# Cross-attention on one core: where the first products of a seven-product block stand against their sums, the order of some loads, and who does the two last steps

## The chip, the cores and the metric

The kernel runs on one core of one Trainium2 chip. A core has a matrix engine, TensorE (PE in the profile, its weight loads PEld), and three engines for everything else: VectorE (DVE), ScalarE (ACT) and GpSimd (POOL). The fifth, SyncE (SP), issues nearly all the DMA transfers here. Each engine works through its own list of instructions in order and waits on semaphores for the others. The metric is the device time in microseconds (us) of one execution.

## The reference, cut to what matters

There are 64 independent blocks. For each, `x` is 256 rows of 512 and the context `c` 256 rows of 384, all in fp32; the weights are shared.

```python
text_p  = x @ W_text  + b_text                   # 256 x 512
audio_p = c @ W_audio + b_audio                  # 256 x 512
Q = layer_norm(text_p,  g1, beta1)
K = layer_norm(audio_p, g2, beta2)
alpha = softmax(Q @ K.T / sqrt(512))             # 256 x 256
h = (alpha @ audio_p) @ W_out + b_out            # 256 x 512
out = layer_norm(h + x, g_out, beta_out)
```

## The kernel before

The kernel does not form `alpha @ audio_p` with the projected context. It multiplies `alpha` with the rows of `c` (the result is called z), and `W_audio @ W_out`, worked out once at the start (`wao`), does the rest; the biases are likewise folded into one row `bao`. A block so has five pieces of work for TensorE: q (x to queries), k (c to keys), sc (scores), z (exponentials times c) and y (z times `wao`).

The pieces q, k and y are done by `Blocks`: a product of matrices cut in two by two is made from seven products of half size, with sums of operands ahead (`sum_x`, `sum_c`, on GpSimd: `xsum`, `csum`, `zsum`; `weight_sums` for the weights) and sums of results behind. Seven products go to four PSUM banks: (1, 6), (2, 5), (3, 4) and (7). `products(...)` issues the matmuls, `leave(...)` issues the sums by which VectorE takes a product out of its bank (line 490): `leave(1)` reads the half bank of product 1, `leave(6)` that of product 6, `leave(2, 5)` and `leave(3, 4)` a whole bank each. Where the program has `leave(1)` ahead of product 6, product 6, which writes to the same bank, waits for that sum. A matmul of fp32 operands is issued in two passes, so a product over one chunk of 128 is two entries of the profile.

The order of work is written out by hand: the scheduler is off (`manual_schedule`), so each engine's instructions stand in the order in which the program calls them. Before the loop, block 0 is projected in the plain way (`Projection`) and block 1 by `Blocks`, among the work on the weights. The last lines there are, in this order: `q[1].products(1, 2)`, `leave(1)`, the turn of q[0], its scaling (`affine`), the other products and sums of q[1], the rest of the weights' work, and the store and re-fetch of q[1].

The loop runs over b from 0 to 61. In iteration b the kernel does the scores of block b, q and k of block b + 2 (held in `q2` and `k2`), z and y of block b - 1 (`last`), and the output layer norm of block b - 2 (`done`). [...]To turn a matrix the kernel loads it in squares of 32 (`squares`, four DMAs, line 88) and lets VectorE transpose the squares (`turn`, line 91, and line 442 for keys). For x and c that is a load from the inputs (`load_x`, `load_c`: `xq`, `cq`; issued in iteration b for block b + 4, and turned by `turn_next(b + 3)`); the queries, keys and exponentials are first written to memory (`qd`, `kd`, `ed`) and fetched back as squares (`qq`, `kq`, `eq`). `turn_e` turns the exponentials. `load_rows(b + 1)` loads block b + 1's x and c as rows: c for z, x for the residual sum `add_x`, which comes two iterations after that block's scores. All these DMAs stand in SyncE's one queue; the rows `go` and `beo` (`g_out` and `beta_out` over all partitions) are loaded through it ahead of the loop.

Buffers bind the order further: most SBUF tiles have two buffers, the x and c rows three, and PSUM's eight banks are six in a ring for products (`p_pj`) and two for scores and z (`p_at`).

After the loop the blocks 62 and 63 are finished by hand, in a stretch in which the exponentials of the last two are turned by TensorE and not through memory (`transpose_e`), and y is made by plain matmuls (`multiply`, `multiply_halves` for the last tile). There the layer norm is: `evict` (VectorE: multiply by the reciprocal of the softmax sum, add x, take mean and variance, lines 638, 267, 268), `scales` (GpSimd: add epsilon, line 344, and raise to the power of -1/2, line 346), `shift` (VectorE: subtract the mean, multiply by `go`, line 704) and `settle` (VectorE: multiply by the scale, add `beo`, line 709; `settle_halves`, line 692, for the last tile), then `store` (line 719, or 695 for the halves).

Of the kernel before, what the change touches and what calls it, by code (L numbers as in the profile page):

```python
# [9 lines left out]
F32 = mybir.dt.float32  # L10
AF = mybir.ActivationFunctionType
ALU = mybir.AluOpType
# [3 lines left out]
P = 128  # L16
SQ = 32
NQ = P // SQ
EPS = 1e-05
# [3 lines left out]
def kernel(  # L23
# [41 lines left out]
    nc = tc.nc  # L65
    ctx.enter_context(tc.manual_schedule())
    B, L, D = x.shape
    S, DA = c.shape[1:]
    H = w_text.shape[1]
    LT, ST = L // P, S // P  # L70
# [4 lines left out]
    xin = ctx.enter_context(tc.tile_pool(name="xin", bufs=3))  # L75
# [20 lines left out]
    def load_c(b):  # L96
        cq = blk.tile([P, S // SQ, DA // NQ], F32, tag="cq", name=f"cq_{b}")
        squares(cq, c[b])
        blocks[b] = [cq]

    def load_x(b):
        xq = blk.tile([P, L // SQ, D // NQ], F32, tag="xq", name=f"xq_{b}")
        squares(xq, x[b])
        blocks[b].append(xq)

    def load_squares(b):
        load_c(b)
        load_x(b)

    def load_rows(b):  # L110
        x_sb = xin.tile([P, LT, D], F32, tag="x", name=f"x_{b}")
        c_sb = cin.tile([P, ST, DA], F32, tag="c", name=f"c_{b}")
        nc.sync.dma_start(x_sb, x[b].rearrange("(t p) d -> p t d", p=P))
        nc.sync.dma_start(c_sb, c[b].rearrange("(t p) d -> p t d", p=P))
        return x_sb, c_sb

    ident = const.tile([P, P], F32, tag="ident", name="ident")
    make_identity(nc, ident)
# [13 lines left out]
    def row(v, name):  # L132
        t = const.tile([P, H], F32, tag=name, name=name)
        nc.sync.dma_start(t, v.rearrange("(o h) -> o h", o=1).broadcast_to([P, H]))
        return t
# [4 lines left out]

    x_0 = xin.tile([P, LT, D], F32, tag="x", name="x_0")
    c_0 = cin.tile([P, ST, DA], F32, tag="c", name="c_0")
    c_rows, x_rows = [v[0].rearrange("(t p) d -> p t d", p=P) for v in (c, x)]
    wa_sb = const.tile([P, AC, H], F32, tag="wa", name="wa")
    wt_sb = const.tile([P, DC, H], F32, tag="wt", name="wt")

# [2 lines left out]
        for q in range(NQ):  # L149
            queues[q].dma_start(t[q * SQ : (q + 1) * SQ, lo : lo + n], v[q, :, lo : lo + n])  # L150

    nc.sync.dma_start(c_0[:, :1], c_rows[:, :1])
    weight_chunks(wa_sb, w_audio, 0, 1, [nc.scalar, nc.sync, nc.scalar, nc.sync])
    weight_chunks(wa_sb, w_audio, 1, 2, [nc.sync] * NQ)
    nc.sync.dma_start(c_0[:, 1:], c_rows[:, 1:])
    for t in range(LT):
        nc.sync.dma_start(x_0[:, t, :], x_rows[:, t, :])
    weight_chunks(wt_sb, w_text, 0, 2, [nc.sync] * NQ)
    ba_sb = row(b_audio, "ba")
    weight_chunks(wt_sb, w_text, 2, 2, [nc.sync] * NQ)  # L160
# [123 lines left out]
    H2 = H // 2  # L284
# [53 lines left out]
    def rstd_of(var, n, total=False):  # L338

        ve = small.tile([P, n], F32, tag="ve", name="ve")  # L340
        if total:
            nc.gpsimd.tensor_scalar(ve, var, 1.0 / D, EPS, ALU.mult, ALU.add)
        else:
            nc.gpsimd.tensor_scalar(ve, var, EPS, None, ALU.add)  # L344
        r = small.tile([P, n], F32, tag="rstd", name="rstd")
        nc.gpsimd.tensor_tensor(r, ve, nhalf[:, :n], ALU.pow)  # L346
        return [r[:, t : t + 1] for t in range(n)]
# [157 lines left out]
    class Attention:  # L505
        def __init__(self, b):
            self.b, self.qT, self.kT = b, q.pop(b).T, k.pop(b).T
            self.xb, self.c_sb = rows[b]

        def scores(self, end=False):  # L510
            if end:
# [84 lines left out]

        def add_x(self):
            for t in range(LT):
                nc.gpsimd.tensor_tensor(self.y[:, t, :], self.y[:, t, :], self.xb[:, t, :], ALU.add)  # L599

        def statistics(self):

# [34 lines left out]
        def evict(self, t):  # L637
            nc.vector.scalar_tensor_tensor(  # L638
                self.y[:, t, :],
                self.ps_y.pop(t),  # L640
                self.rden[:, t : t + 1],
                self.xb[:, t, :],
                ALU.mult,
                ALU.add,
            )
            moments(self.mv, self.y[:, t, :], t)

        def scales(self, lo=0, n=LT):
            self.r = getattr(self, "r", {})
            self.r.update({lo + t: r for t, r in enumerate(rstd_of(self.mv[:, lo : lo + n, 1], n))})  # L650

        def moments(self, tiles=range(LT)):
            if 0 in tiles:
# [20 lines left out]
        def evict_halves(self, t):  # L674
            st = small.tile([P, 2, 6], F32, tag="st2", name="st2")
            for h in range(2):
                half = self.y[:, t, bass.ts(h, H2)]
                nc.vector.scalar_tensor_tensor(
                    half,
                    self.ps_h[h],  # L680
                    self.rden[:, t : t + 1],
                    self.xb[:, t, bass.ts(h, H2)],
                    ALU.mult,
                    ALU.add,
                )
                nc.vector.bn_stats(st[:, h, :], half)
            nc.vector.bn_aggr(self.mv[:, t, :], st)
# [46 lines left out]
    def turn_next(b):  # L734
        xT[b] = turn_x(b)
        xs[b] = sum_x(xT.pop(b))
        cT[b] = turn_c(b)
        cs[b] = sum_c(cT.pop(b))

    def add_bias(b):  # L740
        xb = rows[b][0]
        for t in range(LT):
            nc.gpsimd.tensor_tensor(xb[:, t, :], xb[:, t, :], bao_sb, ALU.add)

    assert B > 3
    q, k, xT, cT, rows = {}, {}, {}, {}, {0: (x_0, c_0)}


    c_turn = RowTurn(c_0, AC, "cT")
# [77 lines left out]
    k[0].affine(g2_sb, be2_sb)  # L827
    part = bias_parts()
    q[1] = Blocks("q", 1, xs.pop(1), wt_blocks, bt_sb)
    q[1].products(1, 2)  # L830
    q[1].leave(1)
    q[0].turn()
    q[0].affine(g1_sb, be1_sb)
    q[1].products(6, 5)
    q[1].leave(6)
    q[1].leave(2, 5)
    q[1].products(3, 4)
# [13 lines left out]
    q[1].normalise()  # L851
    q[1].store()
    q[1].fetch()
    go_sb = row(g_out, "go")
    beo_sb = row(beta_out, "beo")

    done = last = None
    for b in range(B - 2):
        three = b + 3 < B
        at = Attention(b)  # L860
        at.scores()
        if done:
            done.o.leave(3, 4)
            done.o.leave(7)
            done.add_x()
        if last:
            last.turn_e()
        if three and b:
            turn_next(b + 3)
        at.maxima()  # L870
        at.exponentials()
        if not b:
            k[1].turn()
        q2 = q[b + 2] = Blocks("q", b + 2, xs.pop(b + 2), wt_blocks, bt_sb)
        q2.products(1, 6)
        q2.leave(1)
        q2.leave(6)
        at.reciprocals()
        at.divide_e()
        if not b:  # L880
            k[1].affine(g2_sb, be2_sb)
        if b:
            q[b + 1].fetch()
            k[b + 1].fetch()
        at.store_e()
        if b + 4 < B:
            load_squares(b + 4)
        at.fetch_e()
        rows[b + 1] = load_rows(b + 1)
        if done:  # L890
            done.statistics()
        q2.products(2, 5)
        q2.leave(2, 5)
        q2.products(3, 4)
        q2.leave(3, 4)
        q2.products(7)
        q2.leave(7)
        q2.square()
        q2.scales()
        q[b + 1].turn()  # L900
        if not b:
            turn_next(3)
        if done:
            done.shift(0)
            done.shift(1)
        if last:
            last.context()
        q[b + 1].affine(g1_sb, be1_sb)
        if b:
            k[b + 1].turn()  # L910
            k[b + 1].affine(g2_sb, be2_sb)
        if done:
            done.settle(0)
            done.settle(1)
            done.store()
        q2.normalise()
        q2.store()
        if last:
            last.start_products()
        k2 = k[b + 2] = Blocks("k", b + 2, cs.pop(b + 2), wa_blocks, ba_sb)  # L920
        k2.products(1, 6)
        k2.leave(1)
        k2.leave(6)
        k2.products(2, 5)
        k2.leave(2, 5)
        k2.products(3, 4)
        k2.leave(3, 4)
        k2.products(7)
        k2.leave(7)
        k2.square()  # L930
        k2.scales()
        k2.normalise()
        k2.store()
        if last:
            last.o.products(1, 6)
            last.o.leave(1)
            last.o.leave(6)
            last.o.products(2, 5)
            last.o.leave(2, 5)
            last.o.products(3, 4)  # L940
            last.o.products(7)
        done, last = last, at
# [2 lines left out]
    at = Attention(B - 2)  # L945
    q[B - 1].fetch()
    k[B - 1].fetch()
    rows[B - 1] = load_rows(B - 1)
    at.scores()
    done.o.leave(3, 4)  # L950
    done.o.leave(7)
# [11 lines left out]
    add_bias(B - 1)  # L963
    at.transpose_e()
    at.copy_e()
    last.o.products(1, 2)
    q[B - 1].turn()
    last.o.leave(1)
    last.o.products(4)
    q[B - 1].affine(g1_sb, be1_sb)  # L970
    k[B - 1].turn()
    last.o.products(6, 5)
    last.o.leave(6)
    last.o.leave(2, 5)
    k[B - 1].affine(g2_sb, be2_sb)
    done.settle(0)
    last.o.products(3)
    last.o.leave(3, 4)
    last.o.products(7)
# [23 lines left out]
    at.multiply(1)  # L1003
    at.shift(0)
    at.evict(1)
    at.scales(1, 1)
    at.settle(0)
    end.context()
    end.start_output()
    end.multiply(0)  # L1010
    at.shift(1)
    at.settle(1)
    at.store()
    end.evict(0)
    end.scales(0, 1)
    end.multiply_halves(1)
    end.shift(0)
    end.evict_halves(1)
    end.scales(1, 1)
    end.shift(1)  # L1020
    end.settle(0)
    end.store(0, 1)
    end.settle_halves(1)

# [31 lines left out]
```

## Time and profile before

| what | us |
|---|---|
| median of 3 runs (lowest, highest) | 1424.07 (1423.77, 1424.16) |
| the profiled execution, its own time | 1425.29 |
| its span in the profile | 1423.5 |
| PE busy | 1407.9 |
| DVE busy | 1232.9 |
| ACT busy | 932.8 |
| POOL busy | 875.9 |

One execution was profiled; the sums below are made from it. Its own time is 1.8 us more than its span, and 1.2 us more than the median of the runs. A row of the timeline gives the start, the time from the first to the last of the merged instructions, the engine, the line, the operation with output and inputs, and in brackets how long the engine was idle before it and what ended that. The chain of waits is followed back from the last instruction, and shows which engine's work set the end. The granted clock is the share of full speed that TensorE's clock gate let through. Ends of matmuls are modelled by the profile, and GpSimd's times are rough.

### The profile page before, as it was taken

How to read it: one execution, taken by the hardware profiler on the slowest of the kernel's cores; microseconds unless marked ns; L12 is line 12 of the kernel's file. 1: busy time of each engine (PE TensorE's matmuls, PEld its weight loads, DVE VectorE, ACT ScalarE, POOL GpSimd, SP SyncE). 2: the span in 40 equal slices, each digit the busy share in tenths (PEclk: the TensorE clock that was granted, in tenths of full speed). 3: DMA queues.
4: the chain of work that ended last, by engine and by line, in shares of the span. 5: the costliest groups of instructions: out<-in, count | busy, mean ns of one | idle time of the engine just before them, and what ended most of it. 6: DMA issues, size and time to landing. Idle time of an engine off the chain costs nothing.

```text
span 1423.5 us, 22648 instructions
## 1 busy us (share of the span) xinstructions
PE 1407.9 (99%) x6441; PEld 1223.2 (86%) x6441; DVE 1232.9 (87%) x1758; ACT 932.8 (66%) x2293; POOL 875.9 (62%) x1295
## 2 busy tenths in 40 slices
PE   9899999999999999999999999999999999999997
PEld 5688888888888888888888888888888888888885
DVE  5688988988889889889889889888888898898888
ACT  4576766766766766766766767667667667667662
POOL 4566576576566566666666665765665666666645
PEclk9999999999999999999999999999999999999999
DMA  8797788888877887887787887888888778788763
GB/s 195 190 263 236 228 228 238 237 226 236 241 221 231 225 240 233 222 239 234 216 247 231 220 245 230 223 243 237 219 240 244 218 234 236 225 235 231 221 191 116
DMA packets 450578, 322.57 MB, mean 227 GB/s; under 512 B 154900, under 2 KB 382996, under 8 KB 450452
## 3 DMA queue, kind: packets, MB, share of 16 engines
q1 hardware_dynamic: 450356, 320.98, 79.4%
q8 instruction: 52, 0.85, 0.3%
q14 instruction: 74, 0.61, 0.2%
q10 hardware_dynamic: 96, 0.13, 0.0%
HBM read 204.09 MB, written 116.92 MB: 226 GB/s over the span
## 4 chain that ended last, share of the span: by engine, by line
PE 97%; DVE 1%; DMA 1%; POOL 0%; issue 0%; ACT 0%; POOLq 0%; SPq 0%; DVEq 0%
PE ps_q L478 27%; PE ps_k L478 21%; PE ps_y L478 21%; PE ps_sc L517 16%; PE ps_z L583 11%; PE ps_wao L245 1%; PE ps_q L365 1%; DMA c<-in_ctx_dram 0%; DVE part L233 0%; DMA wa<-in_L_xattn_W_audio_dram 0%; PE ps_k L365 0%; DVE st L267 0%; DVE y L638 0%; POOL ve L344 0%; POOL rstd L346 0%
## 5 line engine op out<-in xcount | busy, mean ns | idle before, releaser
L490 DVE TENSOR_TENSOR qr<-ps_q,qr 128x512 f32<-128x512 f32 x252 | 174.2, 691 | 93.9 <-PE ps_q L478 91.5
L517 PE MATMUL ps_sc<-kT,qT 128*128 128x256 f32 x1024 | 231.5, 379 | 0.0
L344 POOL TENSOR_SCALAR ve<-var 128x2 f32<-128x2 f32 x126 | 43.9, 348 | 296.3 <-ACT junk L383 296.3
L517 PEld LDWEIGHTS ps_sc<-kT,qT 128*128 128x128 f32 x1024 | 194.6, 190 | 26.8 <-issue 0.5
L534 ACT ACTIVATE e<-ps_sc,nmx 128x256 f32<-128x256 f32 x128 | 59.5, 469 | 232.6 <-DVE nmx L527 232.6
L478 PE MATMUL ps_q<-wtsum,xsum 128*128 128x256 f32 x756 | 195.7, 382 | 4.7 <-DVE qr L490 4.7
L599 POOL TENSOR_TENSOR yr<-yr,x 128x512 f32<-128x512 f32 x124 | 155.9, 1280 | 71.1 <-DVE yr L490 71.1
L490 DVE TENSOR_TENSOR kr<-ps_k,kr 128x512 f32<-128x512 f32 x252 | 174.3, 692 | 22.5 <-DVE kr L490 0.9
L490 DVE TENSOR_TENSOR yr<-ps_y,yr 128x512 f32<-128x512 f32 x248 | 171.5, 692 | 22.0 <-DVE yr L490 0.9
L478 PE MATMUL ps_k<-wa,cT 128*128 128x256 f32 x630 | 177.1, 379 | 0.0
L583 PE MATMUL ps_z<-eT,c 128*128 128x256 f32 x768 | 176.5, 379 | 0.1
L478 PE MATMUL ps_y<-wao,zT 128*128 128x256 f32 x620 | 174.1, 379 | 0.0
L346 POOL TENSOR_TENSOR rstd<-ve,nhalf 128x2 f32<-128x2 f32 (+1 forms) x194 | 159.4, 821 | 16.1
L478 PEld LDWEIGHTS ps_q<-wtsum,xsum 128*128 128x128 f32 x756 | 144.7, 192 | 24.9 <-issue 5.0
L583 PEld LDWEIGHTS ps_z<-eT,c 128*128 128x128 f32 x768 | 145.9, 190 | 20.7 <-ACT e L534 0.5
L449 ACT ACTIVATE qT<-qT,columns 128x256 f32<-128x256 f32 x256 | 132.8, 591 | 5.8 <-DVE qT L91 5.8
L478 PEld LDWEIGHTS ps_k<-wa,cT 128*128 128x128 f32 x630 | 119.6, 190 | 16.2
L449 ACT ACTIVATE kT<-kT,columns 128x256 f32<-128x256 f32 x256 | 132.1, 587 | 1.4 <-DVE kT L91 1.1
L478 PEld LDWEIGHTS ps_y<-wao,zT 128*128 128x128 f32 x620 | 117.7, 190 | 15.9
L411 ACT ACTIVATE kr<-kr,rstd 128x512 f32<-128x512 f32 x126 | 84.1, 714 | 70.5 <-POOL rstd L346 70.5
L383 ACT ACTIVATE junk<-kr 128x512 f32<-128x512 f32 x126 | 79.4, 630 | 77.1 <-DVE kr L490 72.7
L709 DVE SCALAR_TENSOR_TENSOR yr<-yr,rstd,beo 128x512 f32<-128x512 f32 x124 | 128.7, 1075 | 0.6 <-POOL rstd L346 0.6
(150 smaller groups left out, 2980.7 us busy)
## 6 DMA issues: line engine op xcount, KB each, us to landing
kd<-kr SPq DMA_DIRECT2D x64, 512.0 KB, 3.1
kq<-kd SPq DMA_DIRECT2D x256, 128.0 KB, 3.3
qd<-qr SPq DMA_DIRECT2D x64, 512.0 KB, 4.4
qq<-qd SPq DMA_DIRECT2D x256, 128.0 KB, 3.3
xq<-in_x_dram SPq DMA_DIRECT2D x252, 128.0 KB, 3.0
x<-in_x_dram SPq DMA_DIRECT2D x63, 512.0 KB, 4.0
out_dram<-yr SPq DMA_DIRECT2D x62, 512.0 KB, 4.8
cq<-in_ctx_dram SPq DMA_DIRECT2D x252, 96.0 KB, 2.4
```

The costliest lines, as they stand in the source:

```text
L344: nc.gpsimd.tensor_scalar(ve, var, EPS, None, ALU.add)
L346: nc.gpsimd.tensor_tensor(r, ve, nhalf[:, :n], ALU.pow)
L383: nc.scalar.activation(junk, self.rows[:, t, :], AF.Square, scale=1.0 / math.sqrt(H), accum_out=self.var[:, t : t + 1],)
L411: nc.scalar.mul(row, row, self.r[t])
L449: nc.scalar.activation(self.T[:, k, :], self.T[:, k, :], AF.Identity, bias=bet[:, k : k + 1], scale=gam[:, k : k + 1],)
L478: nc.tensor.matmul(place, lhsT=side, rhs=w, start=(i == 0), stop=(i == len(pairs) - 1))
L490: add = lambda o, i0, i1: nc.vector.tensor_tensor(o, i0, i1, ALU.add)
L517: nc.tensor.matmul(self.sc[:, t, :], lhsT=self.qT[:, k, bass.ts(t, P)], rhs=self.kT[:, k, :], start=(k == 0), stop=(k == HC - 1),)
L534: nc.scalar.activation(self.e[:, t, :], self.sc[:, t, :], AF.Exp, bias=self.nmx[:, t : t + 1], accum_out=self.den[:, t : t + 1],)
L583: nc.tensor.matmul(ps[:, j, :], lhsT=self.c_sb[:, s, bass.ts(lo + j, P)], rhs=self.eT[:, s, :], start=(s == 0), stop=(s == ST - 1),)
L599: nc.gpsimd.tensor_tensor(self.y[:, t, :], self.y[:, t, :], self.xb[:, t, :], ALU.add)
L709: nc.vector.scalar_tensor_tensor(self.y[:, t, :], self.y[:, t, :], self.r[t], beo_sb, ALU.mult, ALU.add)
```

## The change

Five things change.

1. For q[1] ahead of the loop, and for the y of block 61 after it, all products of the first two banks are issued before the first sum. TensorE's order of matmuls stays as it was; what changes is which sums stand ahead of which product in the program. VectorE's order changes with it: the turn of q[0] now stands ahead of the sums of q[1]; after the loop, the turn of the last keys stands ahead of the first sum, and `done.settle(0)` ahead of that turn.
2. In the loop, `turn_next` stands ahead of `last.turn_e`.
3. In iteration 0 the squares of the exponentials are fetched ahead of `load_x`, and behind it in the later iterations as before.
4. x's rows of block b are loaded in iteration b and not in b - 1; the last iteration loads two blocks' rows. The loads of `go` and `beo` move from ahead of the loop into iteration 1.
5. At the end, `scales` of a single tile becomes `scale_soon`, where VectorE adds epsilon and GpSimd does the power alone (three times), and two of the `settle` become `settle_beside`: ScalarE multiplies by the scale and GpSimd adds `beo`.

```diff
-    def load_rows(b):
-        x_sb = xin.tile([P, LT, D], F32, tag="x", name=f"x_{b}")
-        c_sb = cin.tile([P, ST, DA], F32, tag="c", name=f"c_{b}")
-        nc.sync.dma_start(x_sb, x[b].rearrange("(t p) d -> p t d", p=P))
-        nc.sync.dma_start(c_sb, c[b].rearrange("(t p) d -> p t d", p=P))
-        return x_sb, c_sb
+    def load_x_rows(b):
+        x_rows[b] = xin.tile([P, LT, D], F32, tag="x", name=f"x_{b}")
+        nc.sync.dma_start(x_rows[b], x[b].rearrange("(t p) d -> p t d", p=P))
+
+    def load_c_rows(b):
+        c_rows[b] = cin.tile([P, ST, DA], F32, tag="c", name=f"c_{b}")
+        nc.sync.dma_start(c_rows[b], c[b].rearrange("(t p) d -> p t d", p=P))
...
+        def scale_soon(self, t):
+
+            r = small.tile([P, 1], F32, tag="rone", name="rone")
+            ve = small.tile([P, 1], F32, tag="veone", name="veone")
+            nc.vector.tensor_scalar(ve, self.mv[:, t, 1:2], EPS, None, ALU.add)
+            nc.gpsimd.tensor_tensor(r, ve, nhalf[:, :1], ALU.pow)
+            self.r = getattr(self, "r", {})
+            self.r[t] = r
+
+        def settle_beside(self, t):
+
+            row = self.y[:, t, :]
+            nc.scalar.mul(row, row, self.r[t])
+            nc.gpsimd.tensor_tensor(row, row, beo_sb, ALU.add)
...
-    q[1].products(1, 2)
-    q[1].leave(1)
+    q[1].products(1, 2, 6, 5)
     q[0].turn()
     q[0].affine(g1_sb, be1_sb)
-    q[1].products(6, 5)
+    q[1].leave(1)
     q[1].leave(6)
     q[1].leave(2, 5)
     q[1].products(3, 4)
...
-    go_sb = row(g_out, "go")
-    beo_sb = row(beta_out, "beo")
...
+        if three and b:
+            turn_next(b + 3)
         if last:
             last.turn_e()
-        if three and b:
-            turn_next(b + 3)
...
         if b + 4 < B:
-            load_squares(b + 4)
-        at.fetch_e()
-        rows[b + 1] = load_rows(b + 1)
+            load_c(b + 4)
+        if not b:
+            at.fetch_e()
+        if b + 4 < B:
+            load_x(b + 4)
+        if b:
+            at.fetch_e()
+            load_x_rows(b)
+        if not three:
+            load_x_rows(b + 1)
+        load_c_rows(b + 1)
+        if b == 1:
+            go_sb = row(g_out, "go")
+            beo_sb = row(beta_out, "beo")
...
-    last.o.products(1, 2)
+    last.o.products(1, 2, 4, 6, 5)
     q[B - 1].turn()
+    q[B - 1].affine(g1_sb, be1_sb)
+    done.settle(0)
+    k[B - 1].turn()
     last.o.leave(1)
-    last.o.products(4)
-    q[B - 1].affine(g1_sb, be1_sb)
-    k[B - 1].turn()
-    last.o.products(6, 5)
     last.o.leave(6)
     last.o.leave(2, 5)
     k[B - 1].affine(g2_sb, be2_sb)
-    done.settle(0)
...
     at.evict(1)
-    at.scales(1, 1)
+    at.scale_soon(1)
     at.settle(0)
     end.context()
     end.start_output()
     end.multiply(0)
     at.shift(1)
-    at.settle(1)
+    at.settle_beside(1)
     at.store()
     end.evict(0)
-    end.scales(0, 1)
+    end.scale_soon(0)
     end.multiply_halves(1)
     end.shift(0)
     end.evict_halves(1)
-    end.scales(1, 1)
+    end.scale_soon(1)
     end.shift(1)
-    end.settle(0)
+    end.settle_beside(0)
     end.store(0, 1)
     end.settle_halves(1)
```

## The prediction

> **What bounds the kernel now.** I read the page first, then the chain of waits, then the waits of TensorE (PE), then the timeline of the two places where PE is not full. The page and the chain, stage by stage in one iteration of the main loop (start, length, what):
>
> ```profile
> PE 1407.9 (99%) x6441; PEld 1223.2 (86%) x6441; DVE 1232.9 (87%) x1758; ACT 932.8 (66%) x2293; POOL 875.9 (62%) x1295
> ...
> PE 97%; DVE 1%; DMA 1%; POOL 0%; issue 0%; ACT 0%; POOLq 0%; SPq 0%; DVEq 0%
> ```
>
> ```profile
> 697.21 6.04 PE ps_q L478 x28
> 703.25 2.59 PE ps_z L583 x12
> 705.84 4.75 PE ps_k L478 x22
> 710.59 4.75 PE ps_y L478 x22
> 715.34 3.45 PE ps_sc L517 x16
> ```
>
> The five pieces add up to 21.58 us and the next begins where the last ends: in the loop PE is full, and an edit there can only lose. PE's 15.6 us without work (1423.5 - 1407.9) lie at the two ends. The largest, as the list of waits has it (engine, line, what it waited for, total, times, longest), and in PE's own timeline:
>
> ```profile
> PE ps_q L478 <- DVE qr L490: 4.7, 1, 4.7
> ```
>
> ```profile
> 35.42 1.89 PE L478 MATMUL ps_q<-wt,xT 128*128 128x256 f32 x8
> 41.96 3.75 PE L478 MATMUL ps_q<-wtsum,xsum 128*128 128x256 f32 x8 [4.65 <-DVE qr L490]
> ```
>
> Around it, GpSimd's (POOL's) sum for product 6, then the turn of the queries on VectorE (DVE) and their scaling on ScalarE (ACT), all from the timeline:
>
> ```profile
> 37.16 0.72 POOL L308 TENSOR_TENSOR xsum<-xsum,xT 128x256 f32<-128x256 f32 x1
> ```
>
> ```profile
> 42.70 1.25 DVE L91 STREAM_TRANSPOSE qT<-qq 128x1024 f32<-128x1024 f32 x1 [0.89 <-DMA qq<-qd]
> ...
> 43.98 2.08 ACT L449 ACTIVATE qT<-qT,columns 128x256 f32<-128x256 f32 x4 [3.30 <-DVE qT L91]
> ```
>
> The chain from there to the first scores, and the windows (stretch, length, busy us and count of PE, PEld, DVE, ACT, POOL, then clock, DMA share, GB/s):
>
> ```profile
> 41.96 7.34 PE ps_q L478 x20
> ...
> 53.59 3.45 PE ps_sc L517 x16
> ```
>
> ```profile
> 41.96:47.40 5.44, 5.44 (x13) 4.36 (x14) 2.63 (x3) 2.08 (x4) 0.00 (x0) 0.50 0.96 251
> ```
>
> PE stops at 37.31 after products 1 and 2 of q[1]. Its operand for product 6 is there at 37.88 (37.16 + 0.72), but the product shares a bank with product 1, and the sum that empties product 1 runs on DVE only at 41.13 to 41.8, behind four part rows. While PE idles its clock falls to 0.50 and stays there until 47.4: the 20 matmuls take 7.34 us, where the loop's 28 take 6.04, or 0.2157 each, 4.31 for 20.
>
> The end of the run is DVE's and POOL's:
>
> ```profile
> 1418.13 0.77 POOL L344 TENSOR_SCALAR ve<-mvy 128x1 f32<-128x1 f32 x1 [1.32 <-DVE mvy L687]
> ...
> 1418.99 0.93 POOL L346 TENSOR_TENSOR rstd<-ve,nhalf 128x1 f32<-128x1 f32 x1
> 1419.52 0.35 SPq L719 DMA_DIRECT2D out_dram<-y  x1
> ...
> 1420.47 0.83 SPq L695 DMA_DIRECT2D out_dram<-y  x2
> ```
>
> The last power (L346) holds back the two halves, whose stores are the last issues; row 0's store (L719) is out a us before.
>
> **Products before sums (start of the run).** PE's order of instructions does not change; what goes is product 6's wait for DVE. It then waits for POOL alone: 37.95. Products 6 and 5 (8 matmuls, 1.73) end at 39.68; product 3 needs the sum of L310 (POOL, 38.71 + 1.17), so 39.95; its 12 matmuls (2.59) end at 42.54 instead of 49.30. Gain 6.76: about 4 of idle time, and 3.03 of slow clock (7.34 - 4.31), less the 0.27 that product 3 waits.
>
> The clock's part rests on the idle time being short. The trace has idle of 0.57 (before 10.94) with the clock at 1.00, and 3.4 us of idle before the fall near 40.7; 0.64 belongs to the first. The Trainium skill, "TensorE: Matmul & The Clock Gate", Part 1, "What's actually happening", says that a full idle window of about 3.4 us halves the clock, and that about 3.4 us of work restores it. The fall agrees; the return does not, 5.4 us here (41.96 to 47.4). By the page the slow clock costs 1.7 and the gain would be 5.4; I take the measured 3.03.
>
> Next comes 3.43 of ps_wao and 0.86 of ps_bao, to 46.83, then the scores. Their queries are turned at 42.70 (the DMA sets that, so putting the turn ahead of the first sum costs it nothing) and scaled by 46.06: 0.8 us of cover. So scores at 46.83 instead of 53.59.
>
> Does it keep the 6.76? The sums that used to run by 41.8 now wait behind the turn, in DVE's queue: first at 43.95, five of them 3.73 (as `kr` at 66.88: 0.65 + 3.08), last at 47.7. All that hangs on them moves by 2.3 only, against 6.76 for PE. After each name: ready, needed.
> - `xsum` of q[2] (turn 48.9, squares 48.5, rstd 49.6, two adds of 0.73): 51.1, and 51.1. Charge 0.1.
> - `csum` of k[2]: 54.5, and 57.
> - q[1] back from memory: written at 50.95 (54.61 before), fetched from 53.8, last issue 55.1, landing after 2.9 (the median of `qq` at the start, 3.9 the longest): 58.0 to 59.0; turn 1.24, scaled chunks from 59.8 to 62.3; the scores use them from 61.1 to 62.4. Cover: 0 to 1 us.
> - `xq` of block 4: the edit puts e_0's four fetches (1.8 us of SP's queue) ahead of it; it lands near 65.0, and DVE is there at 65.1. If it is 1 us late, maxima and sums are 1 us late, and the banks that PE wants from them (q[3]'s first two sums, about 70) are asked for by the k products at 75.8.
> - e_0 turned: 67.9 (65.1 plus 1.2, 0.9, 0.7), and 70.5. Without fetching it sooner, its fetch would stand behind `xq`, 2 us later, still covered.
> Start: -6.7.
>
> **Loads moved.** x's row load leaves iteration 0 (512 KB) and stands one iteration later; the last full iteration issues two (0.45 us of SP's queue). The two bias rows (256 KB each, 0.45 and 0.43 of SP's queue) stand in iteration 1 instead of ahead of e_0's store; behind them is the store of q[3], which they delay by 0.9, and its consumer is some 10 us away. First use of the rows is iteration 2, of x_1 iteration 3. All 0: SP, where waits of it appear, waits for engines. If this cover were gone it would cost at most the 2.2 us that 512 KB takes at 230 GB/s.
>
> **Turn of x and c ahead of the turn of e (61 iterations).** The e turn (0.70) moves back by 2.06, from about 696.0 to 698.0 at its end; its product is at 703.25. x and c come 0.62 sooner; their fetches were issued by 685.3 and need some 3 us, and the turn is at 695.4. Both are covered, by 5 and 7 us: 0.
>
> **settle(0) and the sums near 1393.** PE's order is the same again. The wait at 1393.46 loses its DVE part, worth 0.2 (the previous matmul was due to end at 1393.27). `settle(0)` goes into DVE's wait for kq (1.40 us until 1394.71) at 1392.75 and fits (0.74 alone, 1.64 at most). But it now runs beside the zsum adds: in the loop a settle takes 1.08 against 0.74 alone, and L324/L325 take 1.18 and 0.90 against 0.73 and 0.46. L325 then ends near 1395.1, and product 3 wanted it at 1394.83. From -0.2 to +0.4; I take +0.1, as the overlap is one settle, not two.
>
> **The two last steps.** DVE loses two settles and gains three adds of one column: not in the trace, nearest L817 (128x4, 0.166), so 0.17; POOL loses three `ve` (0.63 to 0.78) and gains two 128x512 adds (L599, 1.28; 1.72 at most); ACT gains two 128x512 products (L411, 0.71). Going down: evict(0) starts when PE is done, 1413.27 instead of 1413.62; the last mean is ready at 1417.84 (1418.06 before), its `ve` at 1418.0, the power (0.93) at 1419.0 instead of 1419.92. So far 0.9 won. But POOL works in order: the add of row 0 stands behind this last power, 1419.0 + 1.28 (to 1.72) = 1420.3 to 1420.7, and SP's queue holds row 0's store ahead of the two halves. The last issue begins at 1421.07 to 1421.5; it was 1420.88. So +0.2 to +0.6; I take +0.4. If the power takes 0.56 (its least), -0.2.
>
> A rule speaks against this part: the skill's "SBUF — State Buffer", "Who interferes with whom", says that a DVE instruction with two SBUF inputs and a GpSimd one that reads SBUF exclude each other for the whole instruction. By it the power waits for the shift (0.75), and the add for the two halves: last issue near 1422.3, +1.4. The trace shows lengthening of 0.3 to 0.45, not always a full instruction; I keep +0.4 and +1.4 as the bound.
>
> **Sum.** -6.7 + 0.1 + 0.1 + 0.4 = -6.1. The profiled execution took 1425.29 (span 1423.5, 1.8 around it), so 1419.2 for it; it is 1.2 above the median of the runs, 1424.07, and from that: 1418.0.
>
> **Rivals.**
> - q[1]'s way through memory, or block 4's fetch, is later than counted, and PE waits at the scores. For: DMA share is 1.01 at 78 to 100, cover 0 to 1. Against: the DMA engines' share is 0.01 in 51 to 53.6, so the store at 50.95 finds them idle. A landing at 61 costs 2: 1420. Chance 0.10.
> - The edit doesn't do what it says: the wait was not the sum's. Then nothing comes at the start and the end adds 0.5: 1424.6. Against: it ends right when L490 does. 0.04. Or the idle time shortens and the clock falls all the same: 3.0 less, 1421.0; 0.02.
> - Slower: the turn of e waits behind x's turn in every iteration. It decides from the point where x's squares land 12 us late (7 + 5), then each 0.15 us beyond costs 61 x 0.15 = 9, less 6: 1427. Against: SP issues them 10 us ahead. 0.03.
>
> **How the numbers follow.** The likely case has 0.81, its bounds -7.2 (PE's wait 0.2, power 0.56) to -4.6 (rule at the end, settle, xsum each at the worst): 1416.9 to 1419.5. Stretched to the first rival: 1416.7 to 1420.4. This kernel's measurement tells 0.2% (2.8 us) from no change; faster 0.92, same 0.05, slower 0.03.
>
> **What would show it.** Right: ps_q's matmuls without the 4.65, clock 1.00 from 37 to 50, scores near 46.8, iterations of 21.58, POOL's last add after the last power and three stores in a row from 1414 to 1415. Wrong: a PE wait for DMA qq at 61, half clock after 41, a loop piece longer than above, or a last store issued before 1413.8.

## The result, and the profile after

The changed kernel took 1418.68 us (median of 6 runs, 1417.67 to 1419.00), the kernel before 1423.74 in the same series (6 runs, 1423.37 to 1424.16): a ratio of 0.9963, with a 95% interval from 0.995 to 0.9976. That is 5.06 us less; 6.1 were forecast, and 1418.0 as the time. The profiled execution of the changed kernel took 1418.84, with a span of 1417.1.

The page after, its first line of busy times:

```profile
PE 1405.0 (99%) x6441; PEld 1221.0 (86%) x6441; DVE 1232.3 (87%) x1759; ACT 934.6 (66%) x2295; POOL 874.3 (62%) x1294
```

PE is without work for 12.1 us (1417.1 - 1405.0) instead of 15.6, and its busy time is 2.9 shorter with the same 6441 matmuls. Both differences lie at the start (PE's idle time is 3.9 shorter there, and 0.45 longer behind the last scores). The list of waits, PE's rows there (engine, line, what it waited for, total, times, longest):

```profile
PE ps_q L480 <- POOL xsum L310: 1.0, 1, 1.0
...
PE ps_q L480 <- POOL xsum L312: 0.3, 1, 0.3
```

The wait of 4.7 for VectorE's sum is gone, and in its place stand the two waits for GpSimd that the prediction named. PE's timeline, and GpSimd's with the operands it waits for (start, time, engine, line, operation, idle time before it in brackets):

```profile
34.44 1.89 PE L480 MATMUL ps_q<-wt,xT 128*128 128x256 f32 x8
37.34 1.99 PE L480 MATMUL ps_q<-wtsum,xsum 128*128 128x256 f32 x8 [1.00 <-POOL xsum L310]
39.60 1.13 PE L480 MATMUL ps_q<-wt,xsum 128*128 128x256 f32 x4 [0.27 <-POOL xsum L312]
```

```profile
36.33 0.96 POOL L310 TENSOR_TENSOR xsum<-xsum,xT 128x256 f32<-128x256 f32 x1
37.25 1.17 POOL L311 TENSOR_TENSOR xsum<-xT 128x256 f32<-128x256 f32 x1
38.38 1.17 POOL L312 TENSOR_TENSOR xsum<-xT,xsum 128x256 f32<-128x256 f32 x1
```

The chain of waits from there on (start, length, what), and a window over the matmuls that had run at half clock (stretch, length, busy us and count of PE, PEld, DVE, ACT and POOL, then clock, DMA share, GB/s):

```profile
39.60 2.86 PE ps_q L480 x12
42.46 3.43 PE ps_wao L247 x8
45.89 0.86 PE ps_bao L261 x2
46.75 3.45 PE ps_sc L519 x16
50.21 6.04 PE ps_q L480 x28
56.25 4.75 PE ps_k L480 x22
61.00 3.45 PE ps_sc L519 x16
```

```profile
40.00:43.00 3.00, 3.00 (x14) 2.40 (x13) 1.31 (x3) 0.00 (x0) 0.00 (x0) 1.00 0.79 277
```

The clock stays at 1.00, and from 39.60 on PE has no gap up to the second scores.

The end, from the timeline:

```profile
1411.19 0.99 POOL L659 TENSOR_TENSOR rone<-veone,nhalf 128x1 f32<-128x1 f32 x1 [1.81 <-DVE veone L658]
1412.15 1.26 POOL L667 TENSOR_TENSOR y<-y,beo 128x512 f32<-128x512 f32 x1
1412.21 1.87 DVE L709 SCALAR_TENSOR_TENSOR y<-y,rone,beo 128x256 f32<-128x256 f32 x2 [0.44 <-POOL rone L659]
1413.88 0.88 SPq L712 DMA_DIRECT2D out_dram<-y  x2
```

GpSimd's add for row 0 (L667) starts right behind the last power (L659), as forecast. VectorE's two halves (L709), which wait for nothing of GpSimd's but that power, take 1.87 instead of the 0.88 of before:

```profile
1419.96 0.88 DVE L692 SCALAR_TENSOR_TENSOR y<-y,rstd,beo 128x256 f32<-128x256 f32 x2 [0.46 <-POOL rstd L346]
```

The spans can be compared only by stretch, because the same code before the first matmul of q[1] ended at different times in different runs (34.3 to 35.4). The table counts from that matmul; scores 0 and 1 are those of blocks 0 and 1, and the columns come from each run's chain of waits.

| kernel | first matmul of q[1] at | to scores 0 | to scores 1 | scores 1 to the last scores | last scores to the end of the span |
|---|---|---|---|---|---|
| before | 35.42 | 18.17 | 32.42 | 1331.04 | 24.62 |
| after | 34.44 | 12.31 | 26.56 | 1331.03 | 25.07 |
| e1_q_only | 34.87 | 10.82 | 25.90 | 1331.51 | 24.62 |
| e2_all_but_q | 34.76 | 16.81 | 31.06 | 1331.01 | 25.07 |
| e3_old_end | 34.57 | 10.78 | 26.59 | 1331.49 | 24.65 |
| e4_kept_busy | 34.48 | 15.16 | 29.41 | 1331.04 | 24.67 |
| e5_add_first | 34.68 | 11.61 | 25.99 | 1331.47 | 23.96 |
| e6_row0_vector | 35.03 | 10.91 | 25.49 | 1331.03 | 24.05 |
| e7_xsum_first | 34.54 | 10.50 | 25.68 | 1331.48 | 25.00 |
| e8_all | 34.32 | 10.50 | 25.48 | 1331.48 | 24.02 |

Where the stretch from scores 1 to the last scores has 1331.5, scores 1 itself took about 3.9 instead of 3.45, since its queries arrived piece by piece. From before to after: -0.98 (the start of the first matmul; not the change, as e1 and e4, with the code of before up to there, have 34.87 and 34.48), -5.86 (start), -0.01 (loop, and the stretch behind it), +0.45 (end), together -6.40. The change's own part is -5.42; the medians say -5.06.

### The profile page after: what moved, and what is told of

It is laid out like the page before. It is cut to its first block, busy times and chain, and to the rows that moved or that the text cites. A ratio compares the mean times of both kernels' runs of the same rounds, so it can differ in the third digit from the quotient of the medians.

```text
span 1417.1 us, 22773 instructions
## 1 busy us (share of the span) xinstructions
PE 1405.0 (99%) x6441; PEld 1221.0 (86%) x6441; DVE 1232.3 (87%) x1759; ACT 934.6 (66%) x2295; POOL 874.3 (62%) x1294
## 4 chain that ended last, share of the span: by engine, by line
PE 96%; DMA 1%; POOL 1%; DVE 0%; issue 0%; ACT 0%; SPq 0%; DVEq 0%; ACTq 0%; POOLq 0%
PE ps_q L480 27%; PE ps_y L480 21%; PE ps_k L480 21%; PE ps_sc L519 16%; PE ps_z L585 12%; PE ps_y L631 1%; DMA xq<-in_x_dram 1%; DMA x<-in_x_dram 0%; DMA wt<-in_L_xattn_W_text_dram 0%; PE ps_wao L247 0%; DMA wa<-in_L_xattn_W_audio_dram 0%; POOL rone L659 0%; DVE y L709 0%; POOL rstd L348 0%; ACT junk L385 0%
## 5 line engine op out<-in xcount | busy, mean ns | idle before, releaser
L348 POOL TENSOR_TENSOR rstd<-ve,nhalf 128x2 f32<-128x2 f32 x191 | 157.2, 823 | 15.9
L480 PE MATMUL ps_q<-wt,xT 128*128 128x256 f32 x504 | 129.2, 379 | 0.0
```

Source lines behind the costliest of these rows:

```text
L480: nc.tensor.matmul(place, lhsT=side, rhs=w, start=(i == 0), stop=(i == len(pairs) - 1))
```

## The experiments

All were timed in five rounds against the kernel before, in two series, each on a chip of its own (its median 1423.64 in the first, e1 to e4, and 1423.93 in the second, e5 to e8).

**e1_q_only and e2_all_but_q: the order of q[1] alone, and all the rest without it.** e1 is the kernel before with

```diff
-    q[1].products(1, 2)
-    q[1].leave(1)
+    q[1].products(1, 2, 6, 5)
     q[0].turn()
     q[0].affine(g1_sb, be1_sb)
-    q[1].products(6, 5)
+    q[1].leave(1)
```

and e2 is the changed kernel with this edit undone.

> The kernel before with part 1 of the change alone, and of it only the place before the loop: products 6 and 5 of q[1] ahead of the first sum, and the turn of q[0] ahead of the sums. Theory A (the whole gain is made in this place, the moved loads and the order of turns give nothing, the end loses 0.45 us): 5.4 to 6.0 us faster than before, PE's wait there about 1.0 us and for POOL, clock 1.00 throughout, scores of block 0 some 11.4 to 11.6 us after ps_q's first matmul of block 1. Rival B (the loads moved out of the way are needed for PE to keep what it wins): the start wins the same, but PE has to wait at the scores of block 1 or at z of block 0, and 1 to 3 us come back, so 3 to 5 us faster.

> The changed kernel with the order before the loop put back: product 6 of q[1] behind the first sum again; all other parts as changed. Theory A: the idle time of some 4.65 us and the half clock come back, and the end keeps its loss: 0.2 to 0.7 us slower than before. Rival (the moved loads, the order of turns or the blocks after the loop have a share in the gain): faster than before by 0.5 us or more.

e1 took 1418.09 (ratio 0.9959, 0.9947 to 0.9972), e2 1424.08 (1.0002, 0.9993 to 1.0011). So the whole gain is the order of q[1], and all the rest of the change together is worth nothing that the timed runs can tell. The table shows that no gain and loss cancel there: e2's end costs the same +0.45 as after's, and its loop is as long as before's.

PE in e1 waited less for GpSimd than in after, and had scores 0 sooner by 1.49 (10.82 against 12.31). But it hardly kept this to scores 1 (0.66). VectorE's timeline of e1 shows what came instead:

```profile
58.83 1.25 DVE L91 STREAM_TRANSPOSE qT<-qq 128x1024 f32<-128x1024 f32 x1 [2.32 <-DMA qq<-qd]
```

The turn of block 1's queries waited 2.32 us for their fetch from memory, and the scores behind it began late. That is the prediction's first rival, and in e1 it is real. In the changed kernel it did not occur: the same turn began there without a wait, 22.67 us after q[1]'s first matmul, where it began after 23.96 in e1.

```profile
57.11 1.25 DVE L91 STREAM_TRANSPOSE qT<-qq 128x1024 f32<-128x1024 f32 x1
```

PE also came later to scores 1 in after, by its own 1.27 us of waits, so that it would not have noticed a turn as late as e1's.

e2 holds a second reading. It has the wait of before, 4.38 (row below), but its 20 matmuls took 6.24 where before's took 7.34. PE's timeline, the chain, and the windows of e2:

```profile
41.04 3.21 PE L480 MATMUL ps_q<-wtsum,xsum 128*128 128x256 f32 x8 [4.38 <-DVE qr L492]
```

```profile
41.04 6.24 PE ps_q L480 x20
```

```profile
41.50:42.00 0.50, 0.50 (x3) 0.39 (x3) 0.50 (x1) 0.00 (x0) 0.00 (x0) 0.60 0.76 254
42.00:43.00 1.00, 1.00 (x4) 0.82 (x3) 0.99 (x2) 0.40 (x1) 0.00 (x0) 0.50 0.91 265
...
45.00:45.50 0.50, 0.50 (x4) 0.45 (x3) 0.00 (x0) 0.00 (x0) 0.00 (x0) 0.99 1.13 218
```

The clock is at one half from about 41.6 (0.60 over half a us: a fifth of it at full clock) to 45.0, that is 3.4 us. In the kernel before, the edges are these windows:

```profile
40.50:41.00 0.50, 0.00 (x0) 0.00 (x0) 0.50 (x1) 0.18 (x1) 0.00 (x0) 0.78 0.97 225
...
47.50:48.00 0.50, 0.50 (x3) 0.40 (x3) 0.00 (x0) 0.00 (x0) 0.00 (x0) 0.90 1.19 243
```

By the same working it is at one half from 40.8 to 47.6: 6.8 us, twice as long, for nearly the same idle time.

**e3_old_end: the changed kernel with the end of before.**

```diff
-    at.scale_soon(1)
+    at.scales(1, 1)
...
-    at.settle_beside(1)
+    at.settle(1)
...
-    end.scale_soon(0)
+    end.scales(0, 1)
...
-    end.scale_soon(1)
+    end.scales(1, 1)
...
-    end.settle_beside(0)
+    end.settle(0)
```

> The changed kernel with its last steps as before: adding epsilon by GpSimd, both settles by VectorE. Theory A (the end loses because the last add of GpSimd holds row 0's store, and VectorE's two halves with it): 0.3 to 0.6 us faster than the changed kernel, 25.07 us from the last scores' start to the end of the span going to about 24.6. Rival (the end's work is no slower; the 0.45 us are how long the last store takes to land, and differ from run to run): within 0.2 us of the changed kernel.

It took 1419.09 (0.9962, 0.995 to 0.9975), which the timing can't tell from after. By stretch the end is 24.65 against 25.07: the new end costs 0.42. Its start shows the rival again; the turn of block 1's queries waited 3.25, and PE waited with it (from the list of waits):

```profile
PE ps_sc L519 <- ACT qT L451: 1.2, 1, 1.2
```

**e4_kept_busy: the kernel before, with the idle time filled.** Behind product 2 of q[1] stand 17 matmuls of a tile of ones, whose result nobody uses, so that PE's wait for VectorE stays but its idle time does not.

```diff
+    def fill_wait(n):
+        ps = p_at.tile([P, P], F32, tag="at", name="ps_fill")
+        for _ in range(n):
+            nc.tensor.matmul(ps, lhsT=ones, rhs=ones, start=True, stop=True)
...
     q[1].products(1, 2)
+    fill_wait(17)
     q[1].leave(1)
```

> The kernel before, with 17 matmuls of ones (128x128, two passes each, results not used) put behind product 2 of q[1], where PE waits for the sum: some 3.7 us of work for PE that nothing waits for. It takes nothing away of the wait itself, and changes the idle time only. Theory A (the wait costs twice: once as idle time, and once as half clock for 5.4 us behind it): 2.5 to 3.2 us faster than before, clock 1.00 through the next 20 matmuls, which take about 4.3 to 4.6 us instead of 7.3; the scores of block 0 then wait for nothing new. Rival (the clock is not the idle time's doing, or the matmuls behind the wait are slow for want of their operands): no faster than before, the 20 matmuls again over 6 us.

It took 1421.89 (11 runs; 0.9988, 0.9979 to 0.9996). PE's timeline, the chain and a window:

```profile
36.21 3.96 PE L199 MATMUL ps_fill<-ones 128*128 128x128 f32 x34
40.80 1.97 PE L484 MATMUL ps_q<-wtsum,xsum 128*128 128x256 f32 x8 [0.63 <-DVE qr L496]
```

```profile
40.80 4.56 PE ps_q L484 x20
```

```profile
42.00:45.00 3.00, 3.00 (x16) 2.64 (x15) 2.25 (x4) 2.08 (x4) 0.00 (x0) 1.00 1.18 228
```

Product 6 starts no sooner after product 1 than in e2 (6.32 and 6.28), but the 20 matmuls take 4.56 at a clock of 1.00. So the slow clock alone costs 1.68 in e2's run (6.24 - 4.56) and 2.78 in the profiled run of before (7.34 - 4.56). The medians give 1.75 (1423.64 - 1421.89), with an interval of 0.6 to 3.0 that holds both; 2.5 to 3.2 was expected.

**e5_add_first and e6_row0_vector: two other ends.** In e5 the last add of GpSimd is issued ahead of its last power; in e6 VectorE does row 0's last step; epsilon, and the last step of block 62's second tile, stay moved.

```diff
+    end.settle_beside(0)
     end.scale_soon(1)
...
-    end.settle_beside(0)
```

```diff
-    end.settle_beside(0)
+    end.settle(0)
```

> The changed kernel with settle_beside(0) of the last block called ahead of scale_soon(1), so that GpSimd's add of row 0 stands ahead of the last power and not behind it. Theory A (in the changed kernel [...]the first half took 1.48 us instead of 0.48, and row 0's store stands ahead of theirs): the add runs beside the statistics of the halves, from about 18.2 us after the last scores' start, the last power is up to 0.3 us later, the halves take 0.48 and 0.40 again, and from the last scores' start to the end of the span it is 23.9 to 24.3 us instead of 25.07. Rival (the add costs as much wherever it stands, as VectorE has work with two SBUF inputs all the time): 24.8 us or more. The timed runs, 0.8 to 1.1 us, will hardly tell it; the trace does.

> The changed kernel with row 0 of the last block settled by VectorE again (one instruction of 0.74 us behind shift(1)); epsilon stays on VectorE and the power on GpSimd. Theory A (handing epsilon to VectorE wins 0.9 us, and handing row 0 to ScalarE and GpSimd loses more than that): VectorE's 0.74 us lie beside the power of 0.93 to 0.99, the halves begin 0.3 us later than they could, and it is 24.0 to 24.4 us from the last scores' start to the end of the span instead of 25.07. Rival (the loss lies elsewhere, in the stores): 24.8 us or more.

e5 took 1417.91 (0.9959, 0.9945 to 0.9973), e6 1418.00 (0.9959, 0.9946 to 0.9971). Their intervals overlap after's; by stretch both ends are shorter, 23.96 and 24.05 against after's 25.07 and before's 24.62, and the same end repeats within 0.07 in the other kernels of the table. The end of e5 in the timeline:

```profile
1410.33 1.26 POOL L667 TENSOR_TENSOR y<-y,beo 128x512 f32<-128x512 f32 x1 [0.83 <-ACT y L666]
...
1412.58 0.88 DVE L709 SCALAR_TENSOR_TENSOR y<-y,rone,beo 128x256 f32<-128x256 f32 x2 [0.44 <-POOL rone L659]
```

The add now stands in the wait that GpSimd had ahead of its last power (1.81 us in after), and VectorE's halves take 0.88 again. With GpSimd's last add out of the way, what is left of the new end is a gain of about 0.6 (24.62 - 24.05, e6); the add behind the last power turned this into a loss of 0.45.

**e7_xsum_first and e8_all: take the rest of PE's wait at the start.** e7 puts q[1]'s sums of operands ahead of k[1]'s power on GpSimd. e8 is e7 with q[1]'s first two sums ahead of the turn of q[0] as well, so that q[1] is written to memory sooner, and with e5's end.

```diff
+    xs = {1: sum_x(xT[1])}
     k[1].scales()
-    xs = {1: sum_x(xT[1])}
```

```diff
     q[1].products(1, 2, 6, 5)
+    q[1].leave(1)
+    q[1].leave(6)
     q[0].turn()
     q[0].affine(g1_sb, be1_sb)
-    q[1].leave(1)
-    q[1].leave(6)
     q[1].leave(2, 5)
```

> The changed kernel with the sums of x of block 1 on GpSimd ahead of epsilon and power for k[1], in GpSimd's idle time, so that PE's waits for xsum (1.00 and 0.27 us in the changed kernel) go. Theory A (the scores of block 1 are held by the way of q[1] through memory, whose beginning hangs on the sums behind the turn of q[0], and so on a DMA: in all runs so far they began 25.9 to 26.6 us after ps_q's first matmul, whether PE had waited before or not): the scores of block 0 begin 1.2 us sooner, those of block 1 not before 25.7, PE waits there for qT; 0 to 0.6 us faster than the changed kernel. Rival (PE keeps what it wins): 1.2 to 1.4 us faster, block 1's scores 25.2 to 25.4 us after ps_q's first matmul.

> The kernel of e7 with, besides, the first two sums of q[1] ahead of the turn of q[0] in VectorE's order (VectorE waits there 1.69 us for the DMA, the two sums take 1.4), and with the end of e5. Theory A: the other three sums, the squares and the way of q[1] through memory begin 1.4 us sooner, so that the scores of block 1 begin 24.6 to 25.3 us after ps_q's first matmul instead of 26.6, and the end takes 23.9 to 24.3 us instead of 25.07: together 2.0 to 3.0 us faster than the changed kernel. Rival (the sums ahead of the turn delay the turn, and with it the scores of block 0): the scores of block 0 begin later than 11 us after ps_q's first matmul, and no more than the end's 0.8 to 1.1 us is won.

e7 took 1418.50 (0.9964, 0.9952 to 0.9977): PE's wait at the start is gone, scores 0 came 1.81 sooner than in after, scores 1 only 0.88 sooner, because PE waited there for the queries:

```profile
60.22 3.90 PE L519 MATMUL ps_sc<-kT,qT 128*128 128x256 f32 x16 [0.64 <-ACT qT L451]
```

e8 took 1417.06 (1416.34 to 1418.24; 0.9953, 0.9941 to 0.9966), the shortest median of all, with the shortest span, 1415.3; its interval still overlaps after's. It is 1.6 below after, where 2.0 to 3.0 was expected. Its end did what e5's did. Its start did not: e8 issues the store of q[1] 0.6 us sooner after q[1]'s first matmul than e7 (14.08 against 14.69), but scores 1 came only 0.20 sooner. The two chains of waits, e7's first, have the way of q[1] through memory:

```profile
49.23 2.75 DMA qd<-qr
...
53.39 4.77 DMA qq<-qd
```

```profile
48.40 3.69 DMA qd<-qr
...
53.50 4.25 DMA qq<-qd
```

The store took 0.94 longer in e8. SyncE had issued the last of the four fetches of x's squares (512 KB together) only 0.5 us ahead of it, and the DMA engines' share was 1.03 from 48 to 50, against 0.54 in e7. Coming sooner, the store met a transfer that it used to come after. That this is the reason was read from the two traces and not tried by itself.

## Why the prediction was right, point by point

- **Start, -6.7: right in kind, 0.9 too large.** The way to scores 0 became 5.86 shorter against a forecast 6.76. The missing 0.90 splits by the steps of the sum. Product 6's wait for GpSimd was 1.00 and not 0.64 (+0.37 against its place in the forecast): GpSimd's adds began 1.08 after q[1]'s first matmul (0.93 in before), and ran 0.96 and 1.17 beside VectorE's part rows, where the same lines took 0.73 in e1, e3 and e6. The add for product 3 was late by the same cause (+0.26). And the last 12 matmuls took 2.86, not 2.59 (+0.27): the loop's 0.2157 for each leaves out what e4 shows as well, 4.56 for 20 instead of 4.31. That scores 0 began at 46.75, where 46.83 was forecast, is luck: the 0.90 that is missing and the start of q[1] that was 0.98 earlier nearly cancel.
- **The clock's share, 3.03: the term that was mis-sized.** "I take the measured 3.03" was one run's number. It was 2.78 in that run by e4's measure, 1.68 in e2's, and about 1.75 in the medians of e4. The estimate that the prediction drew from the Trainium skill ("TensorE: Matmul & The Clock Gate", Part 1, "What's actually happening") and set aside was 1.7, which is e2's case. Both happen: the half clock lasted 3.4 us in one profile and twice that in the other. The mean clock on record for each timed run points the same way, since 3.4 us more at half clock lower it by 0.0012: of the 21 runs of before in the first series, 9 have 0.996 and 11 have 0.997, with medians of 1423.97 and 1423.20. That these groups are the two cases is not shown, as the idle time at the end lowers the mean too. That PE's idle time would be short enough to keep the clock up was right.
- **q[1] back from memory, cover 0 to 1: right in its steps, and the rival's chance too low.** In after the store was issued 15.54 us after q[1]'s first matmul (15.53 by the forecast), and the last of its four fetches landed 2.84 after its issue (2.9). The first scaled chunk was there 2.0 us before PE used it; 0.9 of this cover is PE's own lateness. But the first rival, given 0.10, came in the other kernels with the new order: in e1, e3, e5, e6, e7 and e8 the turn waited 1.06 to 3.25, and in all of these but e6 the last fetch took 4.25 to 5.30 and scores 1 took 3.90 instead of 3.45. That the DMA engines were shared with the transfers issued right behind does not explain it, since after has the same ones behind as e3 and e5 to e8, at a share of 0.94 from 54 to 56 (0.82 to 1.00 in the six), and landed in time. What the traces have instead is one late part of sixteen (see the last section). That after's profile was spared is luck.
- **xsum of q[2], +0.1; block 4's `xq`; the first turn of e:** VectorE waited 0.48 for `xq`, and PE for none of them. 0.
- **Loads moved, 0: right.** The iterations keep 21.58 (PE's ps_q starts at 690.37 and 711.95), and scores 1 to the last scores 1331.03 against 1331.04.
- **x and c turned ahead of e, 0: right.** The chain in the loop is PE alone, and around 690 the turn of e ends 5.2 us ahead of its product, as forecast. The slower rival did not occur. The turn of e, and PE's next two pieces:

```profile
690.57 0.67 DVE L91 STREAM_TRANSPOSE eT<-eq 128x512 f32<-128x512 f32 x1
```

```profile
690.37 6.04 PE ps_q L480 x28
696.41 2.59 PE ps_z L585 x12
```

- **settle(0), +0.1: 0 by the stretches.** It took 0.92 in VectorE's wait for the keys, of which 0.31 is left; L326 beside it was lengthened to 1.18 as counted, L327 behind it was not (0.45), and PE passes through.
- **Last steps, +0.4: right (+0.45, and e2 the same), with one more wait than counted.** The power took 0.99 (0.93 was taken), and the add 1.26 (1.28). As forecast, row 0's store waited for the add and held SyncE's queue: its issue took 1413.43 to 1413.78, and the halves' stores were issued from 1413.88 on. What the prediction did not have is that the halves were held as well: the first of the two took 1.48 instead of about 0.48, and ended 0.28 after the add, at 1413.69. As row 0's store still stood in the queue then, this cost little more. The rule of the Trainium skill that the prediction weighed ("SBUF — State Buffer", "Who interferes with whom": the shared port pair is an exclusive lock, and the order of issue decides who is blocked) agrees with the halves. The +1.4 that was worked out with it did not come: the power ended 0.41 after the shift beside it, and so did not wait for it and then take its 0.93; and the add began 0.06 ahead of the halves, so that it was they that waited.
- **The sum and the forecast time.** -6.1 was forecast, -5.06 measured by the medians. The two agree within the interval (3.4 to 7.1 us). That the spans differ by 6.40 is no support for the forecast: 0.98 of that is an earlier start of q[1].

## What to carry to other kernels

A wait for a shared bank is cut by issuing all products that need no sum ahead of the first sum; but find the next wait on the same path, because what is won ahead of it can be lost there: e7 came to scores 0 sooner by 1.81 than after and kept 0.88 of it, as the queries were late from memory. A slow-clock stretch in one trace is a sample and not a price: measure the same matmuls with the engine kept busy before crediting a change with it. A step given to GpSimd at the very end belongs in a wait that GpSimd has anyway (e5), not behind its last power, where it holds row 0's store and VectorE's halves.

## What was unexpected of the hardware

- The half clock lasted 3.4 us in e2 and 6.8 in before, after idle times of 4.38 and 4.65. That the clock is set anew every 3.4 us, at times that do not follow the work, would give both: in e2 the fall comes 0.6 after PE has begun to work again, and in before the 3.4 us from 40.8 to 44.2, a third of them idle, did not bring the clock back. This fits the two traces and is not shown; nothing was run that moves the idle time alone.
- An instruction of VectorE with two inputs in SBUF lost a whole microsecond to an add of GpSimd that had started 0.06 earlier (1.48 against 0.48). Other overlaps of the two cost only a part: GpSimd's adds at the start 0.96 to 1.17 instead of 0.73, the shift beside e5's add 1.00 instead of 0.74.
- The code ahead of q[1] ended at 34.3 to 35.4 in ten profiles, though hardly anything of it differs. A comparison of single spans carries that us along.
- One late part of a transfer can undo a schedule. A DMA reports its end in 16 parts in the trace. Of the last fetch of q[1]'s queries, 15 had come by 56.49 in e3 and the last at 59.10; by 56.10 and at 58.16 in e7; all by 56.98 in after. In the six kernels in which the turn waited, one load of instructions (a packet of 16 KB, queue `q8 instruction` in the view of DMAs) starts at 54.6 to 57.0; in after it starts at 56.8, as the queries land, and the late part is that of a fetch of c behind it (by 0.8). Over all ten traces, 276 of the 948 transfers that end within some 3.5 us of such a load have one part over 0.8 us behind the rest, and 109 of the 5352 others. That the load holds up one of the sixteen fits this; no run tried it.
